# Toeplitz coefficients stored with channels innermost, loaded as one run per row

## The chip, the cores and the metric

The kernel runs on one core of a Trainium2 chip. The metric is the device time of one execution in microseconds (us), taken as the median of several runs. Beside the timed runs there is one profiled execution, from which all durations below are read. TensorE is called PE in the profile (its weight loads PEld), VectorE DVE, ScalarE ACT, GpSimd POOL, SyncE SP; "SPq" and "POOLq" are the entries of an engine's queue that issue DMAs.

## The reference, cut to what matters

The model is four residual layers on an image batch x of shape (8, 56, 56, 192). The change lies in layer 0. There a product `qv = q * v` with 576 channels is convolved along the width with a kernel a1 and along the height with a kernel a2, a different kernel for every channel:

```python
p, q, v = silu(x @ p_w.T + p_b), silu(x @ q_w.T + q_b), silu(x @ v_w.T + v_b)
a1 = _rpe_mlp(rpe_input, ...) * decay      # (112, 576): coefficient by offset and channel
a2 = _rpe_mlp(rpe_input, ...) * decay
qv = q * v
o1 = _toeplitz(qv.reshape(b * h, w, D1), a1)                 # along the width
o2 = _toeplitz(transpose(qv, (0, 2, 1, 3)).reshape(...), a2) # along the height
out = (p * (o1 + o2)) @ o_w.T + o_b
```

The reference writes `_toeplitz` with Fourier transforms. It equals a product of each line of 56 positions with a 56x56 Toeplitz matrix, whose entry depends only on the difference of row and column. Layers 1 to 3 (window attention, a depthwise convolution, a selective scan) are not touched by the change.

## The kernel before, in words

**Coefficients.** At the start a small network (pool `rpe`) computes, for each of the two kernels, a tile `rpe_ea` of 96 partitions x 6 blocks x 112 offsets (channels on partitions). One DMA from POOL's queue (L184) writes it to a DRAM tensor `ext` of shape [576, 112]: one row of 112 offsets for each channel. The pool ends there, and the memory that it held is used again by the next stage; the loads of the weights `wqv` (L195) and of the first images (L199) therefore wait until both DMAs to `ext` have landed.

**products.** For each image `qv` is computed and stored in DRAM (L222).

**toeplitz.** This is the stage around the change. It runs over the axis (2), then over 6 blocks of 96 channels (`c0`). One pass of that inner loop is called an iteration here; there are 12 for 4 images. Each iteration does the following.

- It loads `qv` of 4 images as a tile `tzx` (L251): 8 DMAs of 588 KB, each to 56 partitions. Two lines of an image are stacked (u = 0 and 1), so that 112 partitions are in use. On the first axis the run in DRAM is 10752 bytes, on the second 384.
- For each of 4 groups of 24 channels it loads a tile `tm` (L259) with 24 matrices of 112x112. Each matrix is block diagonal, and both diagonal blocks are the same 56x56 Toeplitz matrix; two DMAs of 294 KB fill them, and the rest is set to zero once (L239). The Toeplitz form comes from the address: row p starts one element later than row p-1. There are three `tm` tiles in turn.
- For each channel one fp32 matmul (L263), with the matrix as the stationary operand and a slice of `tzx`, one channel of 112 lines, as the moving operand. The profile counts two weight loads and two matmuls for each of these. Four channels share a PSUM tile, which is copied back over `tzx` by DVE or ACT (L269).
- At the end 8 DMAs of 588 KB on POOL's queue store `tzx` to `o` (L277).

The stage runs twice. The first time, for images 0 to 3, it is alone ("stage one"): three `tzx` buffers, and copies shared by ACT and DVE. The second time, for images 4 to 7 ("stage two"), its steps are mixed into `front(0)`, the layers ahead of the scan for image 0, in an order that the program fixes: two `tzx` buffers, all copies on DVE. The order on each queue is the one in which the recording layer put the instructions: on SP the loads of `tzx` for the next iteration stand behind the last `tm` load of this one, and the `tm` loads of the next iteration stand behind those. A `tm` load waits until the group three before it has left its tile.

After that comes the scan (L991 to L1036), which takes most of the time and holds no Toeplitz work; `front` of the other images runs beside it.

Of the kernel before, what the change touches and what calls it, by code (L numbers as in the profile page):

```python
# [15 lines left out]
F32 = mybir.dt.float32  # L16
# [9 lines left out]
CP = 96  # L26
D1 = 576
CH = 448
NCH = L // CH
TT = 112  # L30
WS, SHIFT, NH, HD = 7, 3, 6, 32
PT_ = WS * 2 * WS
DI, NS, R = 384, 16, 12
ND = DI // 128
NG = 2
NP = NS // NG
SLAB, SLAB_F = 10048, 2688
# [44 lines left out]
def model(ctx: ExitStack, tc: tile.TileContext, a: dict, out: bass.AP):  # L82
    nc = tc.nc
    B = out.shape[0]
    const = ctx.enter_context(tc.tile_pool(name="const", bufs=1))
    dram = ctx.enter_context(tc.tile_pool(name="dram", bufs=1, space=DRAM))

    def load_const(pool, name, eng=None):
        t = pool.tile(list(a[name].shape), F32, name=name + "_sb")
        (eng or nc.sync).dma_start(out=t, in_=a[name])  # L90
        return t

    ident = load_const(const, "ident")
# [2 lines left out]
    nc.vector.memset(eps5, 1e-5)  # L96
    stats0 = const.tile([CP, B, 2, 2], F32, name="stats0")

    ext = [dram.tile([D1, TT], F32, name=f"ext{i}") for i in range(2)]

    qv_d = [dram.tile([D1 // CP, L, CP], F32, name=f"qv{b}") for b in range(B)]
    o_d = [[dram.tile([D1 // CP, L, CP], F32, name=f"o{i}_{b}") for b in range(B)] for i in range(2)]
    x1_d, x2_d, x3_d = ([dram.tile([C, L], F32, name=f"x{i}_{b}") for b in range(B)] for i in (1, 2, 3))
    z_d = [dram.tile([128, ND, L], F32, name=f"z{b}") for b in range(B)]
    zr_d = [dram.tile([128, ND, L], F32, name=f"zr{b}") for b in range(B)]

    xc_d, bc_d = (
        [[dram.tile(shape, F32, name=f"{n}{o}_{b}") for b in range(B)] for o in range(2)]
        for n, shape in (("xc", [128, ND, L]), ("bc", [64, L]))
    )  # L110
    dl_d = [[dram.tile([128, ND, L], F32, name=f"dl{s}_{b}") for b in range(B)] for s in range(4)]
    bmask_d = dram.tile([PT_, 4, 6, PT_], F32, name="bmask_d")
    dg2_d = dram.tile([CP, 2, 9, CP], F32, name="dg2_d")
    dg3_d = dram.tile([128, ND, 9, 128], F32, name="dg3_d")

    def blocks(ap):
        return ap.rearrange("(k p) l -> p k l", p=CP)
# [27 lines left out]
    with tc.tile_pool(name="rpe", bufs=2) as rp, tc.tile_pool(name="rpe_ps", bufs=2, space=PSUM) as rps:  # L145
        pos = load_const(rp, "pos")
        slope = load_const(rp, "slope")
        nc.vector.tensor_scalar(slope, slope, 0.0, 1.0, ALU.max, ALU.min)
        nc.vector.tensor_scalar(slope, slope, 1.0 - 0.95, 0.95, ALU.mult, ALU.add)
        zeros = rp.tile([CP, W - 1], F32, name="zeros")  # L150
        nc.vector.memset(zeros, 0.0)

        decay = rp.tile([CP, 6, TT], F32, name="decay")
        nc.vector.memset(decay, 1.0)
        for c in range(6):
            nc.vector.tensor_tensor_scan(
                decay[:, c, W : 2 * W - 1],
                slope[:, c : c + 1].to_broadcast([CP, W - 1]),
                zeros,
                1.0,  # L160
                ALU.mult,
                ALU.add,
            )
            nc.vector.tensor_copy(decay[:, c, 0 : W - 1], decay[:, c, 2 * W - 2 : W - 1 : -1])
        for i in range(2):
            w0, b0 = load_const(rp, f"t{i}_w0"), load_const(rp, f"t{i}_b0")
            ws, bs = load_const(rp, f"t{i}_ws"), load_const(rp, f"t{i}_bs")
            wo, bo = load_const(rp, f"t{i}_wo"), load_const(rp, f"t{i}_bo")
            h = rp.tile([32, TT], F32, name="rpe_h")
            nc.vector.tensor_scalar(h, pos, w0, b0, ALU.mult, ALU.add)  # L170
            nc.vector.tensor_scalar_max(h, h, 0.0)
            for j in range(3):
                ph = rps.tile([128, 512], F32, name="ps_rpe")
                nc.tensor.matmul(ph[:32, :TT], ws[:, j, :], h, start=True, stop=True)
                h = rp.tile([32, TT], F32, name="rpe_h")
                nc.vector.tensor_scalar(h, ph[:32, :TT], bs[:, j : j + 1], 0.0, ALU.add, ALU.max)
            ea = rp.tile([CP, 6, TT], F32, name="rpe_ea")
            for c in range(6):
                pa = rps.tile([128, 512], F32, name="ps_rpe")
                nc.tensor.matmul(pa[:CP, :TT], wo[:, c * CP : (c + 1) * CP], h, start=True, stop=True)  # L180
                nc.vector.scalar_tensor_tensor(
                    ea[:, c, :], pa[:CP, :TT], bo[:, c : c + 1], decay[:, c, :], ALU.add, ALU.mult
                )
            nc.gpsimd.dma_start(out=blocks(ext[i]), in_=ea)  # L184


    def products(images, beside):
# [38 lines left out]


    def toeplitz(images, beside):
        TC = 24
        G = len(images) * (H // 2)  # L230
        with (
            tc.tile_pool(name="tz", bufs=2) as sp,
            tc.tile_pool(name="tz_t", bufs=1) as tp,
            tc.tile_pool(name="tz_ps", bufs=4 if beside else 8, space=PSUM) as ps,
        ):

            tm = [tp.tile([TT, TC, TT], F32, name=f"tm{i}") for i in range(3)]
            for t in tm:
                nc.gpsimd.memset(t, 0.0)  # L239
            n_t = 0  # L240
            for ax in range(2):
                along_h = "(h u w) c -> u h w c"
                along_w = "(u h w) c -> u w h c"
                stored = "(w u h) c -> u w h c"
                size = dict(h=H, u=2) if ax == 0 else dict(w=W, u=2)
                for c0 in range(D1 // CP):
                    x = sp.tile([TT, G, CP], F32, name="tzx", bufs=2 if beside else 3)
                    for n, b in enumerate(images):
                        v = qv_d[b][c0].rearrange(along_w if ax else along_h, **size)
                        for u in range(2):  # L250
                            nc.sync.dma_start(out=x[u * W : (u + 1) * W, n * 28 : (n + 1) * 28, :], in_=v[u])  # L251
                    for c1 in range(0, CP, TC):
                        t = tm[n_t % 3]
                        n_t += 1
                        e = ext[1 - ax][c0 * CP + c1 : c0 * CP + c1 + TC, :]

                        src = bass.AP(e.tensor, e.offset, [[1, W], [TT, TC], [1, W]])
                        for u in range(2):
                            nc.sync.dma_start(out=t[u * W : (u + 1) * W, :, u * W : (u + 1) * W], in_=src)  # L259
                        for c2 in range(0, TC, 4):  # L260
                            po = ps.tile([TT, 4, G], F32, name="ps_tz")
                            for c in range(4):
                                nc.tensor.matmul(  # L263
                                    po[:, c, :], t[:, c2 + c, :], x[:, :, c1 + c2 + c], start=True, stop=True
                                )
                            cs = slice(c1 + c2, c1 + c2 + 4)
                            copy = nc.vector.tensor_copy if (c2 // 4) % 2 or beside else nc.scalar.copy

                            copy(  # L269
                                x[:, :, cs].rearrange("p (b g) c -> p b g c", g=28)[:, :, ::-1, :],  # L270
                                po.rearrange("p c (b g) -> p b g c", g=28),
                            )
                            yield 1.0
                    for n, b in enumerate(images):
                        v = o_d[ax][b][c0].rearrange(stored if ax else along_h, **size)
                        for u in range(2):
                            nc.gpsimd.dma_start(out=v[1 - u], in_=x[u * W : (u + 1) * W, n * 28 : (n + 1) * 28, :])  # L277
# [8 lines left out]
    with (  # L286
# [8 lines left out]
        nc.vector.tensor_scalar_mul(negA, negA, -1.0)  # L295
        Dsum = wp.tile([128, ND], F32, name="Dsum")
        ones = wp.tile([128, 128], F32, name="ones")
        nc.vector.memset(ones, 1.0 / DI)
        zero2 = wp.tile([128, NG], F32, name="zero2")
        nc.vector.memset(zero2, 0.0)  # L300
# [37 lines left out]
        for i in range(WS):  # L338
            for u in range(2):
                for j in range(WS):  # L340
                    at = (i * 2 + u) * WS + j
                    nc.scalar.dma_start(
                        out=bias[at : at + 1, :, :, u, :],
                        in_=a["table"][:, WS - 1 - i : 2 * WS - 1 - i, WS - 1 - j : 2 * WS - 1 - j].unsqueeze(0),
# [613 lines left out]
        def load_bc(i, k):  # L958
            b, slot, j = chunks[i]
            for ts, name, r0 in ((bms, "bm", 0), (cms, "cm", NS)):  # L960
                ts[i, k] = bcp.tile([128, NG, CH], F32, name=name)
                r = slot % 2 * 32 + r0 + NG * k
                src = bc_d[slot // 2][b][r : r + NG, j * CH : (j + 1) * CH]
                nc.sync.dma_start(out=ts[i, k], in_=src.unsqueeze(0).to_broadcast([128, NG, CH]))

# [383 lines left out]
```

## Time and profile before

| | us |
|---|---|
| median of 3 runs | 22281.97 |
| lowest and highest run | 22275.59, 22308.79 |
| profiled execution, its own time | 22327.07 |
| its span | 22325.3 |
| stage one, first to last matmul of L263 | 523.5 to about 1223 |
| stage two, first to last matmul of L263 | about 2290 to 3476.6 |
| PE busy on L263 (4608 matmuls) | 905.3 |
| PE idle ahead of L263 until a `tm` load landed | 519.0 |

The profiled execution is 0.2% above the median, and what lies outside its span is 2 us. A group of instructions is written as line, engine, operation, output<-inputs, shape. A time after "<-" is what the engine waited for. [...] how many fit in a time is read from a run of matmuls that follow one another, its length divided by its number.

### The profile page before, as it was taken

The numbers are of one execution on the slowest core, as the hardware profiler recorded it, in microseconds if no ns is written. First come the engines' busy times: TensorE is split into PE (matmuls) and PEld (weight loads), VectorE is DVE, ScalarE is ACT, GpSimd is POOL, SyncE is SP. The second block draws the span as 40 slices with busy tenths as digits, with TensorE's granted clock in tenths as the row PEclk, the third lists the DMA queues.
The fourth block names the chain that finished last, engine by engine and source line by source line (L and its number), as shares of the span: only waits on it lengthen the run. The fifth ranks groups of instructions, "written<-read, shape, count | busy, mean of one in ns | idle before, by whom it ended". The sixth has DMA issues, their size and how long they took to land. (4 is left out here: it accounts for less than half of the span.)

```text
span 22325.3 us, 200421 instructions
## 1 busy us (share of the span) xinstructions
PE 18177.3 (81%) x58372; PEld 9602.0 (43%) x58372; DVE 16627.2 (74%) x13276; ACT 12465.2 (56%) x31719; POOL 16168.9 (72%) x8503
## 2 busy tenths in 40 slices
PE   8668867888887888888888888788888888887666
PEld 4545544434443444344443444344434444343223
DVE  2122216997799768987899779976898789967998
ACT  2116114655666475756665566656565666556555
POOL 0000006987789778987898778977898889878999
PEclk9788878999899989999999989998999999998888
DMA  3941676434544455445544464345544564445333
GB/s 93 203 110 46 162 196 161 134 122 160 178 145 127 143 182 155 124 131 179 172 133 122 156 189 145 125 142 179 152 128 129 177 183 125 125 142 189 127 126 109
DMA packets 2666914, 3250.20 MB, mean 146 GB/s; under 512 B 1175646, under 2 KB 2619072, under 8 KB 2634850
## 3 DMA queue, kind: packets, MB, share of 16 engines
q1 hardware_dynamic: 2645588, 3121.12, 47.2%
q0 software_dynamic: 15520, 116.14, 1.4%
q8 instruction: 463, 7.59, 0.1%
q14 instruction: 639, 5.23, 0.1%
q10 hardware_dynamic: 4704, 0.12, 0.0%
HBM read 2661.35 MB, written 575.48 MB: 145 GB/s over the span
## 5 line engine op out<-in xcount | busy, mean ns | idle before, releaser
L991 POOL TENSOR_TENSOR hs<-du,bm 128x896 f32<-128x896 f32 x5376 | 11093.8, 2088 | 78.7 <-DVE ps_a L1015 49.2
L1036 PE MATMUL ps_y<-hc,ident_sb 128*128 128x448 f32 x21504 | 9838.7, 592 | 746.6 <-POOL hc L1021 670.4
L1015 DVE TENSOR_TENSOR_SCAN ps_a<-ps_a,hs 128x898 f32<-128x898 f32 x3360 | 6796.4, 2023 | 803.8 <-ACT ps_a L1006 564.3
L1006 ACT ACTIVATE ps_a<-delta,A_logs_sb 128x449 f32<-128x449 f32 x10752 | 6859.9, 638 | 357.5 <-DVE hs L1015 75.0
L1036 PEld LDWEIGHTS ps_y<-hc,ident_sb 128*128 128x128 f32 x21504 | 4288.2, 207 | 4813.9 <-issue 3557.6
L1021 POOL TENSOR_TENSOR hc<-hs,cm 128x896 f32<-128x896 f32 x2016 | 4038.6, 2003 | 2127.9 <-DVE hs L1015 992.6
L1021 DVE TENSOR_TENSOR hc<-ps_a,cm 128x896 f32<-128x896 f32 x3360 | 3668.8, 1092 | 1220.5 <-PE ps_y L1036 932.5
L1015 DVE TENSOR_TENSOR_SCAN hs<-ps_a,hs 128x898 f32<-128x898 f32 x2016 | 4064.1, 2016 | 327.7 <-ACT ps_a L1006 241.1
L1028 ACT COPY state<-ps_a 128x2 f32<-128x2 f32 x3359 | 528.1, 157 | 3951.9 <-DVE hc L1021 3949.5
L269 DVE COPY tzx<-ps_tz 112x448 f32<-112x448 f32 x432 | 269.9, 625 | 1551.8 <-PE ps_tz L263 1420.2
L277 POOL DMA_DIRECT2D o<-tzx x192 | 97.3, 513 | 1801.3 <-DVE tzx L269 1797.8
L263 PE MATMUL ps_tz<-tzx,tm 112*112 112x112 f32 x4608 | 905.3, 370 | 585.9 <-DMA tm<-ext 519.0
L263 PEld LDWEIGHTS ps_tz<-tzx,tm 112*112 112x112 f32 x4608 | 880.1, 207 | 629.5 <-issue 625.9
L806 PE MATMUL ps_f<-slab 128*128 128x448 f32 x2646 | 1087.5, 547 | 63.9 <-DMA slab<-dg_d 48.7
L996 ACT COPY hs<-state 128x2 f32<-128x2 f32 x4608 | 817.5, 177 | 2.4 <-POOL hc L1021 2.2
L636 PE MATMUL ps_f<-ident_sb,slab 98*98 98x98 f32 x1344 | 331.0, 314 | 570.5 <-ACT slab L629 570.5
L738 PE MATMUL ps_f<-slab 96*96 96x448 f32 x1764 | 723.6, 546 | 39.5 <-DVE slab L725 39.5
L806 PEld LDWEIGHTS ps_f<-slab 128*128 128x128 f32 x2646 | 507.0, 192 | 563.0 <-issue 509.2
L979 POOL TENSOR_TENSOR du<-delta,xcd 128x448 f32<-128x448 f32 x672 | 707.3, 1053 | 23.3 <-DMA slab<-o 23.2
L76 PE MATMUL ps_f<-slab 96*96 96x448 f32 (+6 forms) x2306 | 694.8, 480 | 25.9 <-DMA slab<-dg_d 22.7
L1028 ACT COPY state<-hs 128x2 f32<-128x2 f32 x2016 | 378.9, 188 | 584.6 <-DVE hs L1015 554.8
L621 ACT ACTIVATE slab<-slab,mxs 98x98 f32<-98x98 f32 x1344 | 489.5, 365 | 370.9 <-DVE mxs L618 370.9
(215 smaller groups left out, 17263.1 us busy)
## 6 DMA issues: line engine op xcount, KB each, us to landing
bm<-bc SPq DMA_DIRECT2D x1792, 448.0 KB
cm<-bc SPq DMA_DIRECT2D x1792, 448.0 KB
xcd<-xc SPq DMA_DIRECT2D x840, 224.0 KB
dl<-slab SPq DMA_DIRECT2D x224, 672.0 KB
delta<-dl SPq DMA_DIRECT2D x224, 672.0 KB
tzx<-qv SPq DMA_DIRECT2D x192, 588.0 KB
o<-tzx POOLq DMA_DIRECT2D x192, 588.0 KB, 13.2
slab<-x SPq DMA_DIRECT2D x224, 336.0 KB
```

The costliest lines, as they stand in the source:

```text
L76: return f(*args, **kw)
L263: nc.tensor.matmul(po[:, c, :], t[:, c2 + c, :], x[:, :, c1 + c2 + c], start=True, stop=True)
L738: nc.tensor.matmul(p[:CP, :CH], dg[:, k, t, :], xp[:, u, k, dy : dy + 8, dx : dx + W], start=t == 0, stop=t == 8,)
L806: nc.tensor.matmul(p[:, :CH], dg[:, t, :], xp[:, 8 * j + dy : 8 * j + dy + 8, dx : dx + W], start=t == 0, stop=t == 8,)
L979: nc.gpsimd.tensor_mul(du[:, 0, :], deltas[i][:, d, 1 : CH + 1], xcs.pop((i, d)))
L991: nc.gpsimd.tensor_mul(hs[:, :, tokens(i)[0]], dus[i, d].to_broadcast([128, NG, CH]), bms[i, k])
L996: nc.scalar.copy(hss[g][:, :, tokens(i)[1]], src)
L1006: nc.scalar.activation(dA[:, n, :], deltas[i][:, d, at : at + CH + 1], AF.Exp, scale=negA[:, slot, d, c : c + 1])
L1015: nc.vector.tensor_tensor_scan(h, dA, hs, 0.0, ALU.mult, ALU.add)
L1021: (nc.gpsimd if on_pool(d, k) else nc.vector).tensor_mul(hc, h[:, :, tokens(i)[0]], cms[i, k])
L1028: nc.scalar.copy(states[i][:, d, NG * k : NG * k + NG], h[:, :, tokens(i)[2]])
L1036: nc.tensor.matmul(yps[i, d][:, :CH], ident, hcs[g][:, n, :], start=k + n == 0, stop=k + n == NP + NG - 2)
```

## The change

The DRAM tensor `ext` becomes 24 blocks of shape [112 offsets, 24 channels]: channels innermost. To get there, each `rpe_ea` block of 96 channels is turned over by a matmul with the identity and copied from PSUM by ACT into a tile `eT` with offsets on partitions, and the DMA to `ext` writes runs of 24 channels (96 bytes). In the loop, a row of a `tm` tile (56 columns x 24 channels) is then one contiguous run of 5376 bytes in DRAM and in the tile, where it was 24 runs of 224 bytes. The matrix of one channel is now read from the tile with a step of 24 elements (96 bytes) between its columns, where it was contiguous.

```diff
-    ext = [dram.tile([D1, TT], F32, name=f"ext{i}") for i in range(2)]
+    ext = [dram.tile([D1 // TC, TT, TC], F32, name=f"ext{i}") for i in range(2)]
...
-            nc.gpsimd.dma_start(out=blocks(ext[i]), in_=ea)
+            eT = rp.tile([TT, 6, CP], F32, name="rpe_et")
+            for c in range(6):
+                pt = rps.tile([128, 512], F32, name="ps_rpe")
+                nc.tensor.matmul(pt[:TT, :CP], ea[:, c, :], ident[:CP, :CP], start=True, stop=True)
+                nc.scalar.copy(eT[:, c, :], pt[:TT, :CP])
+            nc.gpsimd.dma_start(
+                out=ext[i].rearrange("n p c -> p n c"), in_=eT.rearrange("p k (n c) -> p (k n) c", c=TC)
+            )
...
-            tm = [tp.tile([TT, TC, TT], F32, name=f"tm{i}") for i in range(3)]
+            tm = [tp.tile([TT, TT, TC], F32, name=f"tm{i}") for i in range(3)]
...
-                        e = ext[1 - ax][c0 * CP + c1 : c0 * CP + c1 + TC, :]
-                        src = bass.AP(e.tensor, e.offset, [[1, W], [TT, TC], [1, W]])
+                        e = ext[1 - ax][(c0 * CP + c1) // TC]
+                        src = bass.AP(e.tensor, e.offset, [[TC, W], [1, W * TC]])
                         for u in range(2):
-                            nc.sync.dma_start(out=t[u * W : (u + 1) * W, :, u * W : (u + 1) * W], in_=src)
+                            dst = t[u * W : (u + 1) * W, u * W : (u + 1) * W, :].rearrange("p i c -> p (i c)")
+                            nc.sync.dma_start(out=dst, in_=src)
...
-                                    po[:, c, :], t[:, c2 + c, :], x[:, :, c1 + c2 + c], start=True, stop=True
+                                    po[:, c, :], t[:, :, c2 + c], x[:, :, c1 + c2 + c], start=True, stop=True
```

More of the change, by code (lines that the diff above doesn't have):

```diff
@@ L34 @@
 ND = DI // 128
+TC = 24
 NG = 2
@@ L228, in toeplitz @@
     def toeplitz(images, beside):
-        TC = 24
         G = len(images) * (H // 2)
```

## The prediction

> **What bounds the kernel now.** I read the groups first: all that the change touches is L263 and its loads. Then the waits, in four stretches that cover the two Toeplitz stages. Here are those of stage one, first axis (engine, line, what it waited for: total us, times, longest):
>
> ```profile
> POOL o L277 <- DVE tzx L269: 325.3, 6, 62.1
> ...
> PE ps_tz L263 <- DMA tm<-ext: 134.6, 8, 37.2
> ```
>
> The second axis has 156.1 us in 6 waits, stage two 67.3 and 161.0. PE waits for coefficients about once per iteration. Next the timeline of an iteration; PE first (start, length, count, idle before it):
>
> ```profile
> 696.23 37.18 PE L263 MATMUL ps_tz<-tzx,tm 112*112 112x112 f32 x192 [20.48 <-DMA tm<-ext]
> 753.70 6.62 PE L263 MATMUL ps_tz<-tzx,tm 112*112 112x112 f32 x33 [20.30 <-DMA tm<-ext]
> ```
>
> ```profile
> 707.07 4.95 SPq L251 DMA_DIRECT2D tzx<-qv  x8
> ...
> 714.99 49.21 SPq L259 DMA_DIRECT2D tm<-ext  x8
> ...
> 734.60 4.05 POOL L277 DMA_DIRECT2D o<-tzx  x8 [53.25 <-DVE tzx L269]
> ```
>
> The period is 753.70 - 696.23 = 57.5 us, of which PE works 37. To see what the DMA engines do in it I cut it in stretches (the columns that matter are the first and the last two: stretch, DMA share, GB/s):
>
> ```profile
> 712.00:734.00 22.00, 21.40 (x112) 21.01 (x110) 4.85 (x8) 3.72 (x7) 0.00 (x0) 1.00 0.90 196
> 740.00:752.00 12.00, 0.00 (x0) 0.00 (x0) 0.00 (x0) 0.00 (x0) 0.00 (x0) 0.50 0.89 353
> ```
>
> The first holds loads of tzx (196 GB/s), the second stores of o (353 GB/s). In the second PE does nothing: the first tm pair of the next iteration is pending. The DMA view of that stretch says why:
>
> ```profile
> DMA packets 921, 4.23 MB, mean 353 GB/s; under 512 B 536, under 2 KB 536, under 8 KB 536
> ```
>
> 385 packets of 10752 bytes pass, and 536 small ones, nearly one for one. A tm packet has 224 bytes, a pair has 2688 of them: while stores pass, a fifth of a pair gets through in 12 us. On the second axis loads alone run at 166 GB/s and tm loads alone (1056 to 1066 us) at 154. So stage one is bound by DMA, and by the way in which small packets share the engines with large ones. Stage two is bound by PE, except for some gaps that end on a tm load.
>
> Last the pitch of the matmuls, since the change alters how weights are read:
>
> ```profile
> 1571.00 4.76 PE L76 MATMUL ps_f<-ident_sb,slab 112*96 112x112 f32 x48
> ```
>
> Contiguous operands: 48 matmuls of 112 columns in 4.76 us less 0.16 of tail, 96 ns each. L263, also 112 columns: (37.18 - 0.18)/192 = 192 ns. Its moving operand has a step of 384 bytes, and I put the factor of two down to that.
>
> [...]
>
> **The change part by part.**
>
> *Coefficient loads, stage one.* A pair goes from 2688 pieces of 224 bytes to 112 of 5376. Bytes are the same. An iteration moves 4.82 MB of tzx, 4.82 MB of o, 2.41 MB of tm. Before, first axis: 4.82/196 + 4.82/353 + 2.41/154 = 24.6 + 13.6 + 15.6 = 53.8 us; the other 3.7 of 57.5 the engines stand idle, after a starved tm has been waited for. Second axis: 29.0 + 13.6 + 15.6 = 58.2 of a period of 63.1 (998.63 to 1061.70). After: tm rows go to the same 56 partitions as the loads, so I take the loads' 196 GB/s: 12.3 us. A tm packet now is half a store packet, so a pair gets its turn within 8 packets of each (14 engines at work, 112/14), some 6.4 us; the idle time goes, as DMA always has something to do. Periods 50.5 and 54.9, gains 7.0 and 8.2. With 11 transitions: 84 us. Late next: tzx loads and stores, which still exceed PE's 37 us. Bounds: nothing, if rows of one block read by 14 engines at once hold each other up; 147 us if rows run at the stores' 353 (11 times 12.8 to 14.0).
>
> *Coefficient loads, stage two.* The gaps that end on tm are 26.4, 36.4, 46.2, some 35 four times, 39.4. Most begin with tzx loads that were issued late, behind instructions of front(0), and these stay late. Only the first, at 2590.5, is starvation by stores: 12 us less. At 2778.8 some 5 go; the other six, and two of 5 us, gain about 14 together by a quicker pair. 31 us. In the built program the changed shape of the loads alters the order of SP's tzx and tm loads among front's DMAs, and of matmuls of L263 among front's, on the second half of stage two; DVE and ACT by a few entries. These are other places for the same waits: 20 us either way.
>
> *Start.* Added: 12 fp32 matmuls with the identity (24 counted by the profile), 12 copies on ACT of 96 elements, and, in the built program, 6 more ACT table loads, one after each pair of copies; the pool has two PSUM banks, so each pair waits for ACT. The DMA to ext becomes 2688 runs of 96 bytes for 576 of 448. This is not hidden:
>
> ```profile
> 19.62 0.76 POOL L184 DMA_DIRECT2D ext<-rpe_ea  x1 [5.36 <-DVE rpe_ea L181]
> ...
> 22.90 0.31 SPq L195 DMA_DIRECT2D wqv<-in_wqv_dram  x1
> 23.64 52.12 SPq L199 DMA_DIRECT2D x<-in_x_dram  x3
> 60.77 4.31 DVE L125 BATCH_NORM_STATS2 gn_st<-x 96x6 f32<-96x448 f32 x8 [41.46 <-DMA x<-in_x_dram]
> ```
>
> SP's next loads, and behind them all of products, wait for the landing at 22.9. For each of two kernels three pairs cost a table load (1.28, from its rows) plus two copies (0.25 each, by the small copies' 0.16 to 0.19) less one table load at the end: 4.5; two make 9. The landing grows from 3.3 by 2.7 (168 pieces per engine at the 16 ns of the smallest tm packets) to 10; I take 5. Sum 14, bounds 9 to 25. POOL's memsets behind it (L202) have 30 us of cover.
>
> *Weights with a step.* 4608 loads of 112 columns with a step of 96 bytes. If the step costs what it costs the moving operand, 112 x 1.7 = 190 ns, which lies beside the matmul's 192: pitch 192 to 195, and 2304 in stage two make 5 us; in stage one PE has 13 us of slack per iteration. Bounds: below nothing is excluded, as the moving operand alone gives 192; above, if the two stepped reads do not run side by side, 380.
>
> *Sum:* -84 - 31 + 14 + 5 = **-96 us**. The profiled 22,327 would become 22,231. It stands 45 above the median, so the median becomes **22,186**.
>
> **The rivals.**
>
> *Weights become the bound (slower).* It starts where a pitch over 192 eats the gain: 84 + 31 - 14 = about 100 us against 2304 matmuls of stage two, so from 44 ns more, 236 ns. At 280 (half overlap): stage two +203, stage one 192 x 0.28 + 2 = 56 per iteration, gain only 45; with -31 and +14 that is +141, median 22,423. At 380 (none): stage two +433, stage one 75 per iteration, +170; +586, median 22,870. For it: no row shows such a load. Against: [...] that L263's pitch is 192 whatever clock is granted, so the array is not what limits it.
>
> *Transfers stay as slow.* If all that changes is packets and the tm data at 154 GB/s was limited by the destination or by one small region of DRAM, the gain is the idle time at most, 3.7 and 4.9 per iteration, less 14 at the start: about -30, 22,250, no change that a measurement tells. Against it: the starved stretch 740 to 752 is no matter of rates.
>
> **How the numbers follow.** Forecast 0.58, its own range 22,090 to 22,235 by the bounds above. Transfers no better 0.10. Weights at about half overlap 0.20, with none 0.12. No change that can be told means within 0.2%, 45 us. Faster 0.58, same 0.10, slower 0.32. The range starts at 22,060 (rows at 353 GB/s and tm gaps of stage two half gone) and goes to 22,500, over the half-overlap case; the no-overlap case and the tails, 0.19, lie outside.
>
> **What would show it.** In the profile after: runs of L263 in stage one still 192 ns each (x192 in some 37 us) or not: this decides the sign. Waits of PE for tm in stage one fall from 291 to about 190 us; periods near 50 and 55. Packets under 512 bytes fall by 258,000. Bytes per us in a stretch of tm loads alone: near 196. The first image statistics (L125) begin near 75 instead of 60.8. A pitch of 236 ns or more, or tm waits as long as before, would prove it wrong.

## The result and the profile after

The changed kernel takes 22185.7 us (median; the kernel before 22282.0 beside it): ratio 0.9959, 95% interval 0.9949 to 0.9969. It is faster by some 0.4%, or 96 us, which is what was forecast. The profiled execution took 22196.5 us, 11 above the median; its span is 22194.7. The lines have moved by 8 or 9: the matmul that was L263 is now L272, the `tm` load L259 is L268, the `tzx` load L251 is L259, the `o` store L277 is L286.

The groups of the changed matmuls and their weight loads (columns as before: busy us, mean ns, then the idle time ahead and what ended it):

```profile
L272 PE MATMUL ps_tz<-tzx,tm 112*112 112x112 f32 x4608 | 1031.6, 403 | 290.5 <-DMA tm<-ext 227.7 <-DMA bc<-slab 48.6 <-issue 14.2
L272 PEld LDWEIGHTS ps_tz<-tzx,tm 112*112 112x112 f32 x4608 | 1028.0, 319 | 329.4 <-issue 323.2 <-DVE tzx L278 0.7
```

Waiting for `tm` has fallen from 519.0 to 227.7 us. But PE is busy for 1031.6 us instead of 905.3, with the same 4608 matmuls. The waits of stage one, both axes:

```profile
POOL o L286 <- DVE tzx L278: 484.6, 10, 66.7
...
PE ps_tz L272 <- DMA tm<-ext: 111.7, 11, 36.4
```

In place of 291 us in 14 waits, PE waits 112 us in 11; in both kernels some 37 of them are for the first load. An iteration in the timeline (start, length, engine, count, idle before):

```profile
574.97 12.76 SPq L268 DMA_DIRECT2D tm<-ext  x4
576.17 4.11 POOL L286 DMA_DIRECT2D o<-tzx  x8 [66.71 <-DVE tzx L278]
587.78 11.00 SPq L259 DMA_DIRECT2D tzx<-qv  x8
602.13 29.95 SPq L268 DMA_DIRECT2D tm<-ext  x8
618.80 42.56 PE L272 MATMUL ps_tz<-tzx,tm 112*112 112x112 f32 x192 [1.61 <-DMA tm<-ext]
```

The 192 matmuls take 42.56 us, a pitch of 221 ns (the median distance of two starts is 220; one matmul is recorded with 403 on average, so successive ones overlap), and PE had been idle for only 1.61 us. The period is 44 us where it was 57.5, and 42.6 of it are PE: on the first axis PE is now the bound. The `o` stores are issued at 576.17 with four `tm` loads just ahead of them on the other queue, the place at which PE used to stand for 20 us. DMA in two stretches of this iteration (last columns: granted clock, DMA share, GB/s):

```profile
576.00:588.00 12.00, 12.00 (x57) 12.00 (x56) 1.88 (x3) 2.13 (x4) 4.11 (x8) 0.50 0.85 295
596.00:608.00 12.00, 12.00 (x57) 12.00 (x56) 2.50 (x4) 1.60 (x3) 0.00 (x0) 0.50 0.89 302
```

The stores (first stretch) no longer stop PE. The second stretch holds loads of `tzx`, which moved at 196 GB/s before and now move at 302. The third column from the right is new too: the granted clock is 0.50 with PE busy for all 12.00 us, where it was 1.00 with PE at work before (712 to 734). The packets of the whole execution:

```profile
DMA packets 2419618, 3250.20 MB, mean 146 GB/s; under 512 B 917598, under 2 KB 2361024, under 8 KB 2387554
```

There are 258,048 fewer small ones, as counted ahead. Last the start:

```profile
28.60 1.32 POOL L191 DMA_DIRECT2D ext<-rpe_et  x1 [9.49 <-ACT rpe_et L190]
34.08 0.31 SPq L204 DMA_DIRECT2D wqv<-in_wqv_dram  x1
...
71.39 4.31 DVE L127 BATCH_NORM_STATS2 gn_st<-x 96x6 f32<-96x448 f32 x8 [47.50 <-DMA x<-in_x_dram]
```

The second `ext` store is issued 9.0 us later than before, lands 5.5 us after that instead of 3.3, and the first statistics start 10.6 us later.

Measured from its first matmul to its last, stage one went from 699.9 to 585.3 us. Stage two, measured here from its first matmul to the first of `front` after it, went from 1152.6 to 1152.5: nothing. (In the kernel before its first matmul starts at 2384.8; the "about 2290" in the table of times ahead is too early.) The first matmul after stage two starts 106 us earlier than before. What follows it, over 18,700 us that the change does not touch, differs by another 24 us in these two profiled executions; the experiments below differ by as much there among themselves, in both directions. So the two profiled executions lie 131 us apart where the medians lie 96 apart.

### The profile page after: what moved, and what is told of

Same layout as the page of the kernel before. It is cut to its first block, busy times and chain, and to the rows that moved or that the text cites. A ratio compares the mean times of both kernels' runs of the same rounds, so it can differ in the third digit from the quotient of the medians.

```text
span 22194.7 us, 200480 instructions
## 1 busy us (share of the span) xinstructions
PE 18380.4 (83%) x58396; PEld 9775.7 (44%) x58396; DVE 16629.6 (75%) x13276; ACT 12479.8 (56%) x31737; POOL 16177.7 (73%) x8503
## 5 line engine op out<-in xcount | busy, mean ns | idle before, releaser
L286 POOL DMA_DIRECT2D o<-tzx x192 | 97.4, 514 | 1686.4 <-DVE tzx L278 1602.9
L272 PE MATMUL ps_tz<-tzx,tm 112*112 112x112 f32 x4608 | 1031.6, 403 | 290.5 <-DMA tm<-ext 227.7
L272 PEld LDWEIGHTS ps_tz<-tzx,tm 112*112 112x112 f32 x4608 | 1028.0, 319 | 329.4 <-issue 323.2
```

What stands on the lines that cost most here:

```text
L272: nc.tensor.matmul(po[:, c, :], t[:, :, c2 + c], x[:, :, c1 + c2 + c], start=True, stop=True)
```

## The experiments

The theory: the rows of 5376 bytes gain more than was forecast, in both stages; reading the weights with a step of 96 bytes costs much of it back, through the pitch and through the granted clock, which slows `front`'s own matmuls in stage two. The rival: the pitch is hidden in stage two, and its gain was lost to other waits there. Ratios are to the kernel before, run on the same chip each time.

### New loads without the step: e1

```
-    t[:, :, c2 + c]
+    tf[:, (c2 + c) * TT : (c2 + c + 1) * TT]        # tf: t as one row of 2688
```

> The changed kernel, except that each matmul of the Toeplitz stages reads its 112 weight columns as one contiguous run of the same tile (so the weights are not the right matrices; loads, packets, stores and the number of instructions are the changed kernel's). Theory one: the step of 96 bytes in the weight read is what takes the pitch from 192 to 220 ns and, through what it does to the granted clock, slows front's matmuls beside stage two. Then the pitch is 192 ns, the granted clock of stage one stands near 0.77 again, front's matmuls go back from 434 to about 375 ns, stage one loses a few more us (its first-axis period falls from 44 to about 40), stage two becomes about 100 us shorter (1152 to 1050), and the time is about 22,070, ratio to the kernel before 0.990 to 0.991. Theory two: the longer pitch is hidden beside other waits (a tm load or front's DMAs take its place in stage two): the pitch is 192, but stage two moves by less than 40 us and the ratio is that of the change, 0.996.

Ratio 0.9908 (0.9892 to 0.9925), 22112.2 us. Pitch 192 ns. PE's waits for `tm` in stage one lie between those of the kernel before (290.7 us) and of the changed kernel (111.7):

```profile
PE ps_tz L273 <- DMA tm<-ext: 161.6, 12, 35.2
```

The two stages in the changed kernel, as stretches (columns: stretch, length, busy time of PE, PEld, DVE, ACT, POOL, granted clock, DMA share, GB/s):

```profile
532.40:1117.70 585.30, 510.03 (x2304) 507.64 (x2304) 89.34 (x143) 76.66 (x144) 44.67 (x88) 0.50 0.86 229
2278.50:3431.00 1152.50, 876.20 (x3162) 682.56 (x3160) 191.60 (x309) 180.04 (x233) 60.53 (x106) 0.69 0.65 185
```

and in e1:

```profile
532.60:1104.80 572.20, 445.81 (x2303) 441.63 (x2304) 89.37 (x143) 76.61 (x144) 44.63 (x88) 0.86 0.88 235
2270.10:3355.20 1085.10, 775.71 (x3162) 594.48 (x3160) 191.69 (x309) 178.40 (x233) 60.47 (x106) 0.81 0.69 197
```

Without the step stage one is 13 us shorter, stage two 67 us, and the clock is back. The rival is out: what stage two had gained by the loads, the step took. Theory one had put 100 us on stage two; 67 came, since PE's waits grew again by 33 us once its matmuls took less.

### The step without the new loads: e2

```
+    tf = t.rearrange("p c i -> p (c i)").rearrange("p (i c) -> p i c", c=TC)
-    t[:, c2 + c, :]
+    tf[:, :, c2 + c]
```

> The kernel before with one edit: each matmul of the Toeplitz stages reads its 112 weight columns with a step of 24 elements through the same tile (so the weights are not the right matrices); the coefficient loads stay as they were, in pieces of 224 bytes. Theory one (the step costs, the loads gain, and the two are separate): pitch 220 ns and a lower granted clock as in the changed kernel; stage one keeps its DMA-bound periods of 57 and 62 us, since 42 us of matmuls still fit in them, so it changes by less than 20 us; stage two becomes 70 to 110 us longer; ratio to the kernel before 1.003 to 1.005. Theory two (the pitch of 220 comes from something else in the changed kernel, for example DMA writes of 5376-byte rows into the tile while it is read): pitch 192 and ratio 1.000.

Ratio 1.0053 (1.0038 to 1.0068), at the upper end of what theory one expected. Pitch 220. The stages, first of the kernel before:

```profile
523.50:1223.40 699.90, 446.36 (x2303) 441.50 (x2304) 89.33 (x143) 76.61 (x144) 44.64 (x88) 0.79 0.89 192
2384.80:3537.40 1152.60, 762.20 (x3161) 587.25 (x3160) 191.43 (x309) 179.34 (x232) 60.48 (x106) 0.79 0.72 187
```

then of e2:

```profile
520.00:1240.20 720.20, 511.58 (x2304) 508.07 (x2304) 89.35 (x143) 76.61 (x144) 44.63 (x88) 0.50 0.88 187
2392.90:3620.60 1227.70, 874.46 (x3161) 679.98 (x3159) 191.45 (x309) 179.68 (x232) 60.42 (x106) 0.67 0.67 175
```

With e1 this makes a square of four kernels:

| stage one / stage two, us | contiguous weights | step of 96 bytes | cost of the step |
|---|---|---|---|
| pieces of 224 bytes | 699.9 / 1152.6 (before) | 720.2 / 1227.7 (e2) | 20 / 75 |
| rows of 5376 bytes | 572.2 / 1085.1 (e1) | 585.3 / 1152.5 (after) | 13 / 67 |
| gain of the rows | 128 / 67 | 135 / 75 | |

The two effects add within 8 us. The tile written by long rows has nothing to do with the pitch: theory two of e2 is out. Both kernels multiply by numbers that are not the right matrices, and the granted clock is high in e1 and 0.50 in e2, so the numbers do not explain it.

Where the step's cost in stage two lies can be read from `front`'s largest group of matmuls there, first before, then after:

```profile
L76 PE MATMUL ps_f<-slab 128*128 128x448 f32 (+2 forms) x661 | 281.9, 573 | 23.0 <-DMA slab<-dg_d 22.7 <-DMA slab<-xc 0.2
```

```profile
L77 PE MATMUL ps_f<-slab 128*128 128x448 f32 (+2 forms) x661 | 318.6, 630 | 6.0 <-DMA slab<-x 3.8 <-DMA slab<-dg_d 1.5 <-ACT slab L77 0.7
```

These are the same 661 matmuls, with nothing changed in them, and they take 57 ns more each. Over the distances between successive matmuls of stage two (each counted up to 1 us, the rest as gap), e1 to after is +60 us for the changed matmuls, +40 for `front`'s (391 to 437 ns on average), and -33 for gaps. That `front`'s part comes from the clock can be read directly. In these traces the granted clock is 1.0 or 0.5 at each moment, and figures between are averages of the two. The starts of successive 128x448 matmuls of `front` lie 376 ns apart (median) at 1.0 and 747 at 0.5, in e1 and in the changed kernel alike; of 459 such distances 46 fall at 0.5 in e1 and 91 in the changed kernel.

### A table of steps: e4

Eight forms of the matmul in one kernel, each with its own step of the weights and of the moving operand. One iteration of each axis in the timeline, first axis with steps (weights, moving) of (1,96), (2,96), (4,96), (24,96) elements, second axis with (1,1), (24,1), (2,1), (8,96):

> A measurement of the step by itself: the changed kernel, where the matmuls of the four channel blocks of each first axis and each second axis read with other steps (weights, moving operand, in elements): first axis (1,96) (2,96) (4,96) (24,96), second axis (1,1) (24,1) (2,1) (8,96). The matrices and, where the moving step is 1, the moving data are not the right ones. Theory one [...]: pitch of (24,1) near 190 to 220, like (24,96); (2,1) between; (1,1) 96 to 100. Theory two (the two reads share something, and only both stepped together are slow): (24,1) near 96 to 110, (1,96) 192, (24,96) and (8,96) and (4,96) 220. [...]

```profile
573.46 9.52 PE L276 MATMUL ps_tz<-tzx,tm 112*112 112x112 f32 x48 [0.51 <-DMA tm<-ext]
582.80 9.46 PE L278 MATMUL ps_tz<-tzx,tm 112*112 112x112 f32 x48
592.09 10.05 PE L280 MATMUL ps_tz<-tzx,tm 112*112 112x112 f32 x48
601.96 10.76 PE L282 MATMUL ps_tz<-tzx,tm 112*112 112x112 f32 x48
...
920.85 7.91 PE L284 MATMUL ps_tz<-tm 112*112 112x112 f32 x48 [24.56 <-DMA tm<-ext]
928.59 10.81 PE L286 MATMUL ps_tz<-tm 112*112 112x112 f32 x48
939.20 5.89 PE L288 MATMUL ps_tz<-tm 112*112 112x112 f32 x48
944.93 10.50 PE L290 MATMUL ps_tz<-tzx,tm 112*112 112x112 f32 x48
```

Median pitch of each form over the whole trace:

| weights, step in bytes | moving, step in bytes | pitch, ns |
|---|---|---|
| 4 | 4 | 98 at clock 1.0, 187 at 0.5 |
| 8 | 4 | 105 at clock 1.0 |
| 96 | 4 | 220 at either clock |
| 4, 8 | 384 | 193 |
| 16 | 384 | 206 |
| 32 | 384 | 211 |
| 96 | 384 | 220 at either clock |

Read beside a contiguous moving operand, the weights alone set 220 ns at a step of 96 bytes. So theory one holds for the step of the change: its weights are slow beside either moving operand, and no sharing of the two reads is needed. A step of 8 bytes costs almost nothing (105 for 98). With 16 bytes the pitch is 206, over the 193 that the moving operand takes, so the step of the weights sets it there too; their time without a stepped moving operand was not run for 16 and 32 bytes. The pitches from 16 bytes on are not equal (206, 211, 220), and 96 bytes is not the only slow step; by what law the step sets the time was not shown.

### The start: e3

```
-    with tc.tile_pool(name="rpe", bufs=2) as rp, ...
+    early = ExitStack()
+    rp = early.enter_context(tc.tile_pool(name="rpe", bufs=2))    # closed after products
```

> The changed kernel with one edit: the SBUF pool of the coefficient network stays open until the first products stage has been issued, so that the loads of wqv and x don't wait for the landing of ext in memory that is to be reused. Theory one: the start is what it looks like, a chain of network, ext, wqv, x; then the first image statistics begin 30 to 40 us earlier than the changed kernel's 71.4, if x is loaded at once, and the time falls by 20 to 40 us (ratio to the kernel before 0.994 to 0.995). Theory two: the first products are bound by something later (ACT or the stores of qv), and the earlier start is given back: statistics earlier, but the first toeplitz matmul stays within 10 us of where it was (532 us) and so does the time.

Ratio 0.9946 (0.9931 to 0.9961); the kernel after had 0.9959, so the times alone do not tell the two apart. The trace does. The timeline of the start:

```profile
8.99 54.74 SPq L210 DMA_DIRECT2D x<-in_x_dram  x3
...
30.73 1.32 POOL L193 DMA_DIRECT2D ext<-rpe_et  x1 [9.47 <-ACT rpe_et L192]
47.51 4.31 DVE L127 BATCH_NORM_STATS2 gn_st<-x 96x6 f32<-96x448 f32 x8 [21.48 <-DMA x<-in_x_dram]
```

`x` no longer waits for `ext`; the first statistics come 24 us earlier (30 to 40 were expected), and so does the first Toeplitz matmul (508.8 for 532.4). The stretch from the start to it is a chain, as theory one said, and the memory of the small network's pool was its first link, in the kernel before too.

### Smaller blocks of channels: e5, e6, e8, e10, e11

As 8 bytes of step cost almost nothing in e4 (105 ns for 98), two or three channels innermost could give longer runs without the cost. All of these start from e3:

```
+TK = 2                                              # 3 in e6, 4 in e8, 8 in e10, 12 in e11
-    ext: [D1 // TC, TT, TC]    tm: [TT, TT, TC]               t[:, :, c2 + c]
+    ext: [D1 // TK, TT, TK]    tm: [TT, TC // TK, TT, TK]     t[:, (c2 + c) // TK, :, (c2 + c) % TK]
```

> The kernel e3_start_pool with the coefficients in blocks of 2 channels: a row of a matrix pair is a run of 448 bytes (1344 pieces per tm pair) and the weights are read with a step of 8 bytes. Theory one ([...] the length of the run sets how a tm pair fares among stores, apart from that): pitch 192 to 194, granted clock as with contiguous weights, stage two near 1090 us, stage one between the kernel before (777 us from its first matmul to the next products) and the contiguous-weight kernel e1 (651 us), near 710; ratio to the kernel before 0.993 to 0.995. Theory two (any step halves the rate): pitch 207 to 220, stage two near 1150, ratio 0.997 to 1.000.

> As e5_pairs with blocks of 3 channels: runs of 672 bytes (896 pieces per pair), weights with a step of 12 bytes. Theory one: [...] pitch 192 to 194; stage one near 685 us, stage two near 1088; ratio 0.992 to 0.994. Theory two (only steps of a power of two, or only 4 and 8 bytes, are cheap): pitch over 200. [...]

> As e5_pairs with blocks of 4 channels: runs of 896 bytes (672 pieces per pair), weights with a step of 16 bytes. By the step table: pitch 207, granted clock as with contiguous weights [...], so front's matmuls beside stage two stay near 385 ns; stage two 1085 + 2304 x 14 ns = 1117 us at most; stage one near 670; ratio 0.992 to 0.995. Rival: [...] 0.5 in stage one, stage two near 1145, ratio 0.995 to 0.997.

> The kernel e3_start_pool with blocks of 8 channels: runs of 1792 bytes (336 pieces per tm pair), weights with a step of 32 bytes, and ext written from a tile whose partitions are blocks (16 matmuls with columns of the identity, 16 VectorE copies per network), in runs of 3584 bytes, so that the start isn't held up by small pieces as in e5, e6 and e8. By the step table: pitch 207 to 220, median near 211, clock as with contiguous weights, front's matmuls near 385 ns; stage one about 580 us, stage two about 1130; the first statistics as in e3, near 47.5 us; ratio to the kernel before 0.992 to 0.994. Rival: with all matmuls at this step the clock falls to 0.5 as at 96 bytes; then stage two is near 1150 and the ratio that of e3, 0.9946.

> As e10_blocks_of_8 with blocks of 12 channels: runs of 2688 bytes, step of 48 bytes. [...] pitch lies between e10's 211 and the 220 of 96 bytes, and the time between e10 and e3; if the fall of the granted clock sets in at a pitch, it sets in between 211 and 220 ns, and this run shows 0.5 or 0.9 in stage one. Stage one does not gain from longer runs any more: within 10 us of e10's.

| | run, bytes | step, bytes | pitch, ns | stage one: length, waits for `tm`, clock | stage two: length, clock | ratio |
|---|---|---|---|---|---|---|
| before | 224 | 4 | 192 | 699.9, 291, 0.79 | 1152.6, 0.79 | 1 |
| e5 | 448 | 8 | 193 | 667.6, 253, 0.80 | 1144.9, 0.79 | 1.0009 (1.0001 to 1.0018) |
| e6 | 672 | 12 | 195 | 662.4, 245, 0.80 | 1091.2, 0.82 | 0.9977 (0.9968 to 0.9986) |
| e8 | 896 | 16 | 207 | 590.2, 144, 0.86 | 1116.2, 0.81 | 0.9964 (0.9951 to 0.9977) |
| e10 | 1792 | 32 | 219 | 600.6, 131, 0.70 | 1134.4, 0.76 | 0.9950 (0.9937 to 0.9964) |
| e11 | 2688 | 48 | 234 | 586.7, 79, 0.50 | 1201.5, 0.67 | 0.9980 (0.9972 to 0.9987) |
| e3 | 5376 | 96 | 220 | 576.3, 101, 0.50 | 1150.7, 0.69 | 0.9946 (0.9931 to 0.9961) |

(The expectations of e5, e6, e8 and e7 count stage one up to the next products' first matmul, 77 us more than this table; those of e9, e10 and e11 count as it does.) The pitches of e5, e6 and e8 came as expected or within 1 ns, and their clock stayed up (0.80, 0.80 and 0.86 in stage one), which puts e8's rival, 0.5 there, out. Four expectations failed. First the transfers: between 672 and 896 bytes stage one falls by 72 us (46 of them in the periods of the second axis), more than anywhere else on this list, while from 448 to 672 it falls by 5 where 25 were expected (710 to 685); e5's stage two took 1144.9 us where 1090 were expected. Second the ratios of e5, e6 and e8, in part because of the start: `ext` is then written in pieces of 8, 12 and 16 bytes, by six stores for each network in place of one. The start of e5:

```profile
16.01 6.21 POOL L195 DMA_DIRECT2D ext<-rpe_et  x3 [9.91 <-ACT rpe_et L193]
36.48 2.00 POOL L195 DMA_DIRECT2D ext<-rpe_et  x1 [14.27 <-issue]
...
87.25 4.30 DVE L128 BATCH_NORM_STATS2 gn_st<-x 96x6 f32<-96x448 f32 x8 [61.21 <-DMA x<-in_x_dram]
```

The twelve stores go on past 115 us, and `x`, issued at 9.01, arrives 40 us later than in e3 (51 in e6, 31 in e8); the first Toeplitz matmul starts 53 us later. Whether the size of the pieces or the number of stores does it was not separated. e10 and e11, written from partitions that hold blocks, have their first statistics near 46, but their VectorE copies stand among these, and the first Toeplitz matmul comes 12 and 22 us after that of e3. Third, e10's pitch is 219 where the table of steps had 211, and its clock 0.70, between the two that were expected. Fourth, e11's is 234, over the 220 of twice its step, its clock 0.50, and its time is outside the two that were to enclose it; that it would lie between them was the author's assumption:

```profile
L276 PE MATMUL ps_tz<-tzx,tm 112*112 112x112 f32 x4608 | 1098.5, 419 | 255.4 <-DMA tm<-ext 204.0 <-issue 29.9 <-DMA dl<-slab 21.6
```

Here the loads gain as in the change, and the step takes nearly all of it: stage two is 49 us longer than before. None of the five shows a gain over e3; the intervals of e8 and e10 overlap with its own.

### Turned on the chip: e7, then e9

e7 loads the long rows of the change into two tiles of their own, and a VectorE copy turns each block, one ahead, into the contiguous form that the kernel before read:

```
+    tl = [tp.tile([TT, TT, TC], F32, name=f"tl{i}") for i in range(2)]
+    nc.vector.tensor_copy(tm[m % 3], tl[m % 2].rearrange("p i c -> p c i"))    # a block ahead
-    t[:, :, c2 + c]
+    t[:, c2 + c, :]
```

> The kernel e3_start_pool with the rows of 5376 bytes loaded into two tiles of their own, and a VectorE copy (112 x 2688, one per block of 24 channels, issued a block ahead) that turns each into the three contiguous tiles that the matmuls read. Theory one (the step is the only thing that the changed kernel lost, and VectorE has room for 4 copies of about 3 us in a period of 42): pitch 192, granted clock as in e1, stage one near 650 us, stage two near 1085, start as in e3; time about 95 + 70 + 24 us under the kernel before, ratio 0.990 to 0.991. Rival: the copies, in order behind the evictions on VectorE, come late and PE waits for them: more than 100 us of new waits of PE for VectorE, ratio 0.994 or more.

Ratio 0.9968 (0.9957 to 0.9979): worse than the change. Pitch 192 and clock 0.81, but stage one takes 668.9 us, where theory one means some 573 as counted here. PE's waits in it:

```profile
PE ps_tz L284 <- DMA tzx<-qv: 262.9, 12, 39.8
```

This is neither theory: PE doesn't wait for VectorE. A coefficient load now waits on SP's queue until a copy has freed its tile, and the `tzx` loads of the next iteration stand behind it. e9 issues these an iteration ahead:

```
     n_t += 1
     fetch(n_t + 1)
+    if c1 == 0:
+        load_x(ax * (D1 // CP) + c0 + 1)
```

> The kernel e7_turned_on_chip with the eight loads of each tzx issued one iteration ahead, right after the first coefficient load of the iteration before, so that on SP's queue they no longer stand behind coefficient loads that wait for the VectorE copies. Theory one (in e7 the 313 us for which PE waited for tzx are only this order): these waits go, stage one falls from e7's 669 us to about 575, stage two to about 1085, start as in e3; time 22,080 to 22,110, ratio to the kernel before 0.990 to 0.991, better than the changed kernel's 0.9959 by more than both intervals. Rival (the copies cost what they save: 4 x 3.5 us on VectorE, in order with the evictions, hold the evictions up and so PE's PSUM banks, or the two load tiles are too few): waits for tl or for VectorE of over 100 us in stage one, ratio 0.994 or more.

Ratio 0.9916 (0.9903 to 0.9930), 22118.7 us against 22304.5: 186 us faster than the kernel before, and faster than the change by more than both intervals (some 24 us of it are the start of e3). The stages:

```profile
511.50:1112.50 601.00, 445.72 (x2304) 441.50 (x2304) 248.70 (x190) 76.62 (x144) 106.01 (x88) 0.84 0.82 223
2273.90:3335.80 1061.90, 795.81 (x3162) 598.27 (x3160) 342.81 (x354) 178.22 (x232) 77.26 (x106) 0.80 0.73 201
```

The copies, and PE's waits in stage one:

```profile
L265 DVE COPY tm<-tl 112x2688 f32<-112x2688 f32 x96 | 335.6, 3504 | 274.2 <-DMA tl<-ext 274.2
```

```profile
PE ps_tz L292 <- DVE tm L265: 195.1, 12, 39.8
```

So theory one came out nearly, with stage one at 601 for 575 and the time 9 us over its range, and the rival is half there: its waits of over 100 us came (195, of which 40 are the first load), its ratio did not. PE waits for a copy, whose own wait is for the load, some 6 to 8 us in an iteration of the first axis and 19 to 22 on the second, and stage one is 29 us longer than in e1. Stage two is 23 us shorter than in e1; the `tzx` loads are issued ahead there, but whether that is why was not separated. e9 is the fastest version here that multiplies by the right matrices.

## Why the prediction was right, and where not

The sign, the time and the range held, but by two errors of about 80 us each that cancel; that 96 us were forecast and 96 measured is luck. Term by term, with the square of four kernels:

**Coefficient loads, stage one: predicted -84, measured -128** at the old pitch (e1), -115 with the new one. The mechanism held: PE's waits for `tm` fell from 291 us to 162 (e1) and 112 (after), and the stores no longer hold PE up. The step that failed is the rate: I summed the transfers of an iteration at the rates of before, with 196 GB/s for the loads of `tzx` on the first axis. For `tm` alone that was near (211 in 532 to 535). But the `tzx` loads moved at 302 in the stretch shown, and e1's periods are (741.4 - 532.6)/5 = 41.8 and (1068.0 - 806.9)/5 = 52.2 us instead of 50.5 and 54.9. The bound of 147 had held it. The 196 was thus a figure of that kernel and not of loads to 56 partitions.

The packets in the traces show a little more. A `tzx` row of 10752 bytes took 816 ns (median of the 448 in 696 to 754) before and 508 in e1 (448 in 574 to 616); a row of the stores of `o` takes 404 in both. While `tzx` alone is loaded, the kernel before shows packets of 4 bytes in bunches of 14, 3.1 us apart (712 to 734; the DMA share of 0.90 there is 14.4 of 16 engines), as if one load at a time were under way, to one group of 56 partitions. In the changed kernel they are spread over the time (596 to 608), as if loads to both groups were under way together. That this makes the rate, and that the missing small pieces bring it about, was not tested. One reading of the prediction was also off: of the 536 small packets beside the stores (740 to 752), 423 have 224 bytes and 113 have 4, so a sixth of a pair got through and not a fifth.

**Coefficient loads, stage two: predicted -31, give or take 20; measured -67.** I counted on the late `tzx` loads to stay late and on six gaps to shrink by 14 together. These two steps failed: gaps of over 3 us ahead of PE, up to the first matmul of `front` after the stage, fell from 378 to 268 us in the changed kernel and to 304 in e1. Why they fell so far was not taken apart.

**Weights with a step: predicted +5, measured +13 in stage one and +67 in stage two.** This is the step of the argument that was most wrong: that a weight load of 190 ns would lie beside the moving operand's 192, which was my estimate; no trace of the kernel before showed it. Priced by the moving operand's step it came out just under the bound; it takes 220 by itself (e4), so it became the bound. The upper bound of 380 held it. The rival's own price, 2304 matmuls by 28 ns, gives 65 us for stage two, and 67 were measured, but of other parts: 60 of pitch, 40 of `front`'s matmuls at a lower clock, less 33 of waits that PE would have had anyway. That the changed matmuls slow their neighbours was in no case of mine; I had argued that L263's pitch doesn't depend on the clock, and forgot that those of `front` do.

**Start: predicted +14, measured +11.** The three table loads and copies per network made 9.0 as worked out; the landing added 2.2, not 5.

**Sum:** -128 - 67 + 13 + 67 + 11 = -104, and the first matmul after stage two came 106 us earlier. The forecast was -96.

Of the rivals, "weights become the bound" came true in kind and not in size: 220 ns is above 192 and under the 236 at which it would have turned the sign. With its turn-over at "about 100 us" of gain to eat, it was placed too low, as the true gain was 195, or 184 less the start. e11 shows that side: 234 ns with the clock at 0.50 costs stage two 49 us more than before, and the ratio is 0.998. "Transfers stay as slow" is out. Of the signs that I named, packets (-258,048), the first statistics (71.4 for 75) and `tm` loads alone (211 for 196) came. The waits fell further than named (112 for 190), and the periods too (44 and 50 for 50 and 55). L272 at 192 ns did not come, and I had said that this decides the sign, which was too strong.

## What to carry to other kernels

A layout in DRAM that makes loads long also sets the step with which an engine reads the tile: price both reads, the weights by themselves, since a price that lands just below the bound of its neighbour (190 against 192) is no cover (the pitch became 220). Where a transposed read costs time on the bottleneck, an engine with room can turn the tile once (3.5 us for 2688 elements of each partition here) while the load keeps its long rows. And when waits are moved on a queue, look at what stands behind them: e7 lost over 100 us to order alone.

## What the runs showed of the hardware that was not expected

- fp32 weights of 112 columns, as the pitch of matmuls with a contiguous moving operand: 98 ns contiguous and 105 at a step of 8 bytes (clock 1.0), 220 at 96 bytes at either clock; 220 also beside a stepped moving operand (e4). Beside one it does not rise steadily with the step: 206 to 207 at 16 bytes (e4, e8), 211 to 219 at 32 (e4, e10), 234 at 48 (e11), 220 at 96. Why 48 is worse than 96 was not tried.
- The granted clock fell to 0.50 for the whole of stage one in every kernel with a pitch of 220 or more in all its matmuls (after, e2, e3, e11), was 0.70 at 219 (e10), and 0.79 to 0.86 at 192 to 207. In the changed kernel the 0.50 lasted through runs of 42.56 us without a pause of PE; e2 and the kernel before, whose PE waits in stage one are much alike (245 and 291 us), stand at 0.50 and 0.79. The clock goes with the rate at which matmuls follow one another in these runs; that this is its cause was not isolated.
- Twelve stores in 8-byte pieces (32,256 for each of two tensors) beside `x` put its arrival off by 40 us (e5 against e3).
- The length of runs paid most between 672 and 896 bytes: 72 us of stage one, most of it on the second axis. Why there is open.
